# Cross attention with a sequential scan: the last block's queries transposed like the others', other due dates, and a changed path for the last 256 rows

## The chip, the cores and the metric

The kernel runs on one core of one Trainium2 chip, in a single launch. The metric is the device time of one execution in microseconds (us), as a median over runs. A profiled execution is a further run, with a time of its own. The core's engines are TensorE (PE in the profile; PEld are its weight loads), VectorE (DVE), ScalarE (ACT), GpSimd (POOL) and SyncE (SP), whose queue issues nearly all DMA transfers.

## The reference

`x` has 4096 rows and `ctx` 3202 rows of 512 float32 values; there are 8 heads of 64 and a state of 64. Cut to what matters:

```python
x1 = x + mha(LN1(x), LN1(ctx))             # 8 heads, softmax(q k / 8) v, then W_o and b_o
U  = (LN2(x1) @ W_in.T + b_in) @ Bmat      # 4096 x 64
s  = 0
for t in range(4096):
    s = silu(s @ A.T) + U[t]
    states[t] = s
out = x1 + states @ Cmat + (mean(ctxb) @ W_prog.T + b_prog)
```

## The kernel before

**Preparation.** The context is normalised in chunks, multiplied with the weights of keys and values, and the results are put into DRAM (`kd`, `vd`, lines 577 to 678), from where each unit of attention loads what it needs.

**Units of attention.** The 4096 queries form 8 blocks `Q` of 512. A unit is a block, a pair of heads `hp` and a `half` of 256 queries: 64 units, numbered 0 to 63. In the first seven blocks the two halves of a pair follow each other; in the last block all four pairs of one half come before those of the other, and keys and values are loaded again for each unit. A unit runs over 13 blocks of 256 keys. For each of these TensorE makes scores (16 small matmuls, L706), ScalarE takes the exponential of them with a shift (L783), VectorE adds the result into a running sum (L791) and TensorE multiplies it with the values (16 matmuls, L840). The scores go through a ring of two PSUM tiles, the exponentials through a ring of 18 SBUF tiles, the products into a single PSUM tile. So the work on TensorE is a row of half-steps, scores and products in turn. A unit ends with a copy of the products (L885, ScalarE), a join with what came before (L889, VectorE), a folding of the sums (L798, L810, L815), the sums over keys (L868, TensorE), their copy (L907), the reciprocal (L912) and the scaling (L923), and with the row operations L777 and L915 that belong to the choice of the shift.

**Queries.** `queries()` (L993) loads a block's rows, normalises them (factors on GpSimd, scaling on ScalarE, L981) and transposes them in one of two ways. For blocks 1 to 6 (`mixes(Q)`, L1074) VectorE transposes 32 x 32 squares (the flip, L1057) and four moves per half, each of four DMAs on SP's queue (L1069, 32 KB each), bring the squares to their places. For block 0 and block 7 TensorE transposes (the turn, L296, 8 matmuls for each half), and ScalarE copies the result from PSUM (L319). Either way the products with the query weights follow (heads, L325).

**Rows.** `project()` (L1094) works on a finished block by halves: load x, add a row of biases on GpSimd (row, L1110), product with W_o (outs, L1116), residual (L1129), statistics and scaling, flip, move, the product that gives U (inputs, L1172) and its copy (L1181). The inputs of a half need the moved block, so TensorE waits there for a DMA. A further GpSimd operation adds the constant row of `mod` (L1133).

**Tail.** The scan runs in chunks, in two sweeps. The second, `b`, has 16 steps of a product (z, L1281, TensorE), a tanh (L1309, ScalarE) and a sum (h, L1316, VectorE), which makes the states (L1348) and their products with Cmat (L1355), copied, added and stored (L1369 to L1380). The last 256 rows are finished only here. `last_rows()` (L1441) has their own chain: residual (L1457), statistics (L259, L261), factors (three GpSimd operations, L268 to L272), scaling (L280, ScalarE), turn (L296, L1472), copy (L1477), inputs (L1482), 20 serial steps of z, tanh and h (L1281, L1518, L1521), states (L1530), products with Cmat (L1565) and output (L1568). Beside it run checks: `differ()` (L1394 to L1407) compares two sweeps' states, `risen` looks at the shifts, `counted` and `number` (L1741) make of them a number that decides whether a general path is run afterwards; for these inputs it isn't.

**What sets the order.** The order of instructions on each engine is made when the program is built, by the class `Plan` (L69): every piece is added with an engine, an estimated cost, the pieces after which it may stand, a due date and the buffers that it takes and gives. A list scheduler puts them into one order by these. `SHIFT` (L82) moves the due dates of some kinds of pieces by so many times `STEP`, about one pair of half-steps. `from_(d)` (L957) names the piece of scores that is due at `d`; a piece that stands "after" it is only ordered behind it. On the chip an instruction waits for the data and buffers that it uses, and for what stands ahead of it on its engine.

```python
def mixes(Q):
    return 0 < Q < NQB - 1
```

Of the kernel before, what the change touches and what calls it, by code (L numbers as in the profile page):

```python
# [33 lines left out]
FIRST = 3  # L34
EPS = 1e-5
# [33 lines left out]
class Plan:  # L69
# [114 lines left out]
def xattn_ssm_kernel(  # L184
# [772 lines left out]
    def from_(d):  # L957

        return ("scores", *divmod(min(int(d / STEP), len(steps) - 1), NDC))
# [33 lines left out]
    def queries(plan, Q, d):  # L993

        copied, w = [], {}
        of_xn = ("query", Q, 0, "move0") if mixes(Q) else ("queries", Q, 0, "turn")
        for half in range(2):
            ks = [("query", Q, half * 2 + t) for t in range(2)]
            at = [Q * QB + half * QU + t * P for t in range(2)]
            k2, v = ("queries", Q, half), {}  # L1000
# [6 lines left out]
            for t in range(2):  # L1007
# [5 lines left out]
                             [] if mixes(Q) else [free] * 2, [from_(d + 8 * STEP)])  # L1013
# [10 lines left out]
            def turn(half=half, nv=nv, at=at, v=v, open_=open_):  # L1024
                open_()
                xn = w["xn"][:, :, half * QU : (half + 1) * QU]
                v["turns"] = [turned(xn, nv[t]["xh"], t, f"x{at[t]}") for t in range(2)]
                for one in v["turns"]:
                    next(one)

            after = [of_xn] if half else []
            takes = [] if half else ["xn"]
            if mixes(Q):
                for t in range(2):
                    plan.add((*ks[t], "flip"), "DVE", 720,
                             lambda t=t, v=v, nv=nv: flip(v["x"], nv[t]["xh"], t),
                             [(*k, "scaled") for k in ks], d + 4 * STEP + t, [], [("xh", (*ks[0], "scaled"))])
                for a in range(P // TB):
                    plan.add((*ks[0], f"move{a}"), "SP", 2600, partial(move_, a),
                             [(*k, "flip") for k in ks] + ([(*ks[0], "move0")] if a else after),  # L1040
                             d + (5 + 4 * a) * STEP, [] if a else takes, [free])
                    copied.append((*ks[0], f"move{a}"))
            else:
                plan.add((*k2, "turn"), "PE", 1050, turn, [(*k, "scaled") for k in ks] + after, d + 4 * STEP,
                         ["m", "m"] + takes, [("xh", (*ks[0], "scaled"))])
                for t in range(2):
                    plan.add((*ks[t], "copy"), "ACT", 560, lambda t=t, v=v: next(v["turns"][t], None),
                             [(*k2, "turn")], d + 5 * STEP + t, [], [("m", (*k2, "turn"))])
                    copied.append((*ks[t], "copy"))
# [24 lines left out]
    def mixes(Q):  # L1074
        return 0 < Q < NQB - 1
# [18 lines left out]
    def project(plan, Q, halves, d, index):  # L1094

        for half in halves:
# [157 lines left out]
    def open_scan():  # L1254
# [13 lines left out]
        for name, n in (  # L1268
            ("end0", NCK + 1), ("end1", NCK + 1), ("ul", PRE + 1 + P), ("hw", P), ("hl", P),
            ("sl", P + 1), ("df", NCK), ("thl", P // LT), ("st", P // LT),  # L1270
            ("top", 1), ("low", 1), ("bad", 1), ("badl", 1), ("badr", 1),
        ):
            sv[name] = two[:, at_ : at_ + n]
            at_ += n
# [116 lines left out]
    def largest(new):  # L1391

        top, low = sv["top"], sv["low"]
        nc.vector.tensor_reduce(top, new, AX.X, ALU.max, apply_absolute_value=True)  # L1394
        nc.vector.tensor_scalar(low, top, -TOL, None, ALU.mult)
        nc.vector.tensor_scalar(top, top, TOL, None, ALU.mult)

    def differ(new, old, n, bad):

        top, low, df, ok = sv["top"], sv["low"], sv["df"][:, :n], sv["ok"][:, :n]  # L1400
        nc.vector.tensor_tensor(df, new, old, ALU.subtract)
        nc.vector.tensor_scalar(ok, df, top, None, ALU.is_le)
        yield
        nc.vector.scalar_tensor_tensor(ok, df, low, ok, ALU.is_ge, ALU.mult)
# [36 lines left out]
    def last_rows(plan, d):  # L1441

        n = len(units) - 1
        v = dict(x1={}, xh={}, tp={}, pu={}, fs={})
# [87 lines left out]
        for g in range(2):  # L1532
# [4 lines left out]
            plan.add(("l.stats", g), "DVE", 870, partial(stats_, g), [("l.x1", g)], d + g)  # L1537
            plan.add(("l.factors", g), "POOL", 1100, partial(factors_, g), [("l.stats", g)], d + g)
            plan.add(("l.scaled", g), "ACT", 800, partial(scaled_, g), [("l.factors", g)], d + g)
# [11 lines left out]
        for t in range(PRE + LT):  # L1551
# [3 lines left out]
            plan.add(("l.h", t), "DVE", 180, partial(h_, t), [("l.tanh", t)], d)  # L1555
        plan.add("l.from", "DVE", 180, from_, [("l.h", PRE)], d + 7 * STEP)
# [17 lines left out]
    def neighbours():  # L1574

        sl = sv["sl"]
        nc.vector.tensor_copy(sl[:NS, 0:1], sv["end0"][NS:, END : END + 1])
        nc.vector.tensor_copy(sl[NS:, 0:1], sl[:NS, P:])
# [64 lines left out]
    def drain(plan):  # L1643
# [18 lines left out]
        plan.add("start", "SP", 0, ready_scan, ["fetch", ("sums", n)], d - 2 * STEP, ["s"])  # L1662
        plan.add("yb", "SP", 0, ready_rows, [("den", n - 1, 1)], a0, ["m", "m"])
        plan.add("py1", "SP", 0, ready_py, ["start", ("rise", n)], d, ["s"])
# [21 lines left out]
        plan.add("close", "SP", 0, close, [("l.x1", g) for g in range(2)] + ["py1", ("join", n)] + ended, d - 16 * STEP)  # L1686
# [21 lines left out]
        for name, new, old, count, bad, of in (  # L1708
            ("b", lambda: sv["end0"][:, 1:], lambda: sv["end1"][:, 1:], NCK, "bad", [("b", "end")]),
            ("l", lambda: sv["sl"][:, : P : LT], lambda: sv["st"], P // LT, "badl",  # L1710
             ["l.near", "l.from", ("differ", "b", 2)]),
# [9 lines left out]
            costs = (1250, 500, 440) if count == NCK else (900, 300, 350)  # L1721
            for i in range(3):
                plan.add(("differ", name, i), "DVE", costs[i],
# [3 lines left out]
        def risen():  # L1727
            bad = sv["badr"]
            nc.vector.tensor_scalar(rises, rises, RISE, None, ALU.is_le)
            nc.vector.tensor_reduce(bad, rises, AX.X, ALU.add, negate=True)  # L1730
            nc.vector.tensor_scalar(bad, bad, 3.0 * len(units), None, ALU.add)
# [7 lines left out]
        def number():  # L1739
            sv["nbad"] = small.tile([1, 1], I32, tag="nbad", name="nbad")  # L1740
            nc.vector.tensor_copy(sv["nbad"], sv["py"][1][0][0:1, 0:1])  # L1741
# [4 lines left out]
        plan.add("l.near", "DVE", 320, neighbours, ["l.states", ("b", "end")], d)  # L1746
# [247 lines left out]
```

## Time and profile before

| | us |
|---|---|
| median of three runs | 1957.63 |
| lowest and highest run | 1956.58, 1958.08 |
| profiled execution, its time | 1960.71 |
| profiled execution, its span | 1958.9 |

The mean granted clock of TensorE in the profiled execution was 0.996. The span is what the profiler's records cover. In a row of a timeline stand the start in us from the span's start, the length, the engine, the line, the operation, output and inputs with their sizes, and the number of instructions drawn together; at its end, in brackets, the idle time ahead of it and what ended that. Matmuls overlap, so starts tell more than lengths. In a row of a group the figures after the bar are the busy time in us, the mean length of one in ns, then the idle time ahead and its releasers.

### The profile page before, as it was taken

To read this page: it belongs to the slowest core of one execution; us is meant where nothing else is said; L and a number is where in the kernel's file an instruction comes from. 1 tells how busy PE (TensorE), PEld (TensorE's weight loads), DVE (VectorE), ACT (ScalarE), POOL (GpSimd) and SP (SyncE) were. 2 spreads that over 40 slices of the span, in tenths; PEclk is the share of its full clock that TensorE was granted. 3 is DMA by queue.
4 is the path that set the end of the run, shared out by engine and by line. 5 is a ranking of instruction groups with operands and counts; after the bars stand their busy time and mean duration, and the time that the engine had idled before them with its cause. 6 is when DMAs were issued, how large, how long until landed. Compare 5 with 4: busy or idle time off the path is not lost. (4 is left out here: it accounts for less than half of the span.)

```text
span 1958.9 us, 66935 instructions
## 1 busy us (share of the span) xinstructions
PE 1928.9 (98%) x29092; PEld 1259.3 (64%) x29092; DVE 1459.3 (74%) x1983; ACT 1171.3 (60%) x1632; POOL 225.5 (12%) x374
## 2 busy tenths in 40 slices
PE   9999999999999999999999999999999999999996
PEld 5444577666667666666667666666666666766674
DVE  4321489688878887888868886888778886877876
ACT  2233477566666666666657665666666675665653
POOL 2111000001200120011100120012001100011105
PEclk9999999999999999999999999999999999999998
DMA  6533234123422243223312342224322331544476
GB/s 195 172 102 108 64 85 115 48 86 88 129 79 80 86 114 84 74 83 109 104 47 86 92 121 77 81 87 122 87 82 75 95 96 43 156 134 141 143 207 199
DMA packets 246935, 204.28 MB, mean 104 GB/s; under 512 B 80809, under 2 KB 220073, under 8 KB 246637
## 3 DMA queue, kind: packets, MB, share of 16 engines
q1 hardware_dynamic: 242616, 193.32, 34.1%
q10 hardware_dynamic: 4020, 6.62, 1.1%
q8 instruction: 231, 3.78, 0.8%
q14 instruction: 68, 0.55, 0.1%
HBM read 156.32 MB, written 29.88 MB: 95 GB/s over the span
## 5 line engine op out<-in xcount | busy, mean ns | idle before, releaser
L783 ACT ACTIVATE p<-s,shifts 128x1024 f32<-128x1024 f32 (+1 forms) x832 | 890.1, 1081 | 482.9 <-PE s L706 474.3
L791 DVE TENSOR_TENSOR acc<-p,acc 128x1024 f32<-128x1024 f32 (+1 forms) x704 | 830.5, 1180 | 203.6 <-ACT p L783 169.8
L840 PE MATMUL po<-p,v 64*64 64x256 f32 x12800 | 834.1, 377 | 2.7 <-DVE o L889 2.5
L706 PE MATMUL s<-q,k 64*64 64x256 f32 x12800 | 834.9, 377 | 1.8 <-ACT p L783 1.8
L706 PEld LDWEIGHTS s<-q,k 64*64 64x64 f32 x12800 | 490.4, 133 | 214.2 <-issue 13.3
L840 PEld LDWEIGHTS po<-p,v 64*64 64x64 f32 x12800 | 485.0, 133 | 192.6 <-issue 12.0
L1110 POOL TENSOR_TENSOR xr<-xr,rowb 128x512 f32<-128x512 f32 x30 | 42.7, 1436 | 984.9 <-DMA xr<-in_x_dram 984.9
L912 DVE RECIPROCAL rd<-rd 128x256 f32<-128x256 f32 (+1 forms) x64 | 110.2, 1722 | 13.0 <-ACT rd L907 12.7
L325 PE MATMUL pq<-xn,wq 128*128 128x512 f32 x248 | 110.7, 598 | 0.0
L1116 PE MATMUL pa<-wo,o 128*128 128x512 f32 x240 | 107.0, 599 | 0.0
L623 PE MATMUL pv<-wv,ct 128*128 128x512 f32 (+1 forms) x208 | 92.6, 595 | 0.9 <-DVE wv L406 0.9
L656 PE MATMUL pk<-ct,wk 128*128 128x512 f32 (+1 forms) x224 | 88.9, 550 | 0.0
L575 DVE COPY ct<-tp_c 128x512 f32<-128x512 f32 (+1 forms) x13 | 8.4, 649 | 105.7 <-PE tp_c L296 105.7
L791 DVE TENSOR_TENSOR acc<-p,p 128x1024 f32<-128x1024 f32 x64 | 78.1, 1221 | 10.6 <-ACT p L783 10.6
L325 PEld LDWEIGHTS pq<-xn,wq 128*128 128x128 f32 x248 | 45.7, 190 | 55.5 <-issue 54.3
L1116 PEld LDWEIGHTS pa<-wo,o 128*128 128x128 f32 x240 | 44.4, 190 | 56.0 <-issue 55.5
L815 DVE TENSOR_TENSOR acc<-swap,acc 64x256 f32<-64x256 f32 x126 | 60.5, 480 | 11.1 <-ACT swap L810 9.4
L656 PEld LDWEIGHTS pk<-ct,wk 128*128 128x128 f32 x224 | 39.2, 190 | 42.6 <-issue 42.6
L623 PEld LDWEIGHTS pv<-wv,ct 128*128 128x128 f32 (+1 forms) x208 | 36.8, 186 | 43.4 <-issue 41.1
L664 ACT ACTIVATE ks<-pk,bias 128x512 f32<-128x512 f32 (+1 forms) x28 | 18.0, 642 | 74.7 <-PE pk L656 67.6
L810 ACT COPY swap<-acc 64x256 f32<-64x256 f32 x126 | 50.9, 404 | 16.9 <-DVE acc L798 14.4
L334 ACT ACTIVATE q<-pq,bias 128x512 f32<-128x512 f32 x31 | 21.3, 688 | 62.5 <-PE pq L325 62.5
(222 smaller groups left out, 1217.9 us busy)
## 6 DMA issues: line engine op xcount, KB each, us to landing
k<-kd SPq DMA_DIRECT2D x432, 128.0 KB, 2.3
v<-vd SPq DMA_DIRECT2D x432, 128.0 KB, 2.1
xn<-x SPq DMA_DIRECT2D x416, 32.0 KB, 1.9
xr<-in_x_dram SPq DMA_DIRECT2D x30, 256.0 KB, 3.5
x1d<-xr SPq DMA_DIRECT2D x30, 256.0 KB, 2.2
x<-in_x_dram SPq DMA_DIRECT2D x28, 256.0 KB, 3.2
cx<-in_ctx_dram SPq DMA_DIRECT2D x25, 256.0 KB, 3.3
vd<-vs SPq DMA_DIRECT2D x25, 256.0 KB, 2.4
```

The costliest lines, as they stand in the source:

```text
L325: nc.tensor.matmul(pq, wq[:, i, hp * P : (hp + 1) * P], xn[:, i, :], start=(i == 0), stop=(i == NC - 1),)
L623: nc.tensor.matmul(pv[h * HD : h * HD + n, :H], ct[:, k, o : o + n], wv[:, k, :], start=(i == 0), stop=(i == NC // parts - 1), skip_group_ ...
L656: nc.tensor.matmul(pk[:, :n_g], wk[:, i, hp * P : (hp + 1) * P], ct[:, i, :n_g], start=(i == 0), stop=(i == NC - 1),)
L706: nc.tensor.matmul(s[k0 : k0 + HD, a, b, :], kts[(*w["at"][:2], c)][r, b * CK + k0 : b * CK + k0 + HD], q[r], start=True, stop=True, skip_ ...
L783: nc.scalar.activation(t[:, :, :nb, :], w["ps"][c][:, :, :nb, :], AF.Exp, bias=w["shift"])
L791: nc.vector.tensor_tensor(w["acc"][:, :, :nb, :], t[:, :, :nb, :], before[:, :, :nb, :], ALU.add)
L810: nc.scalar.copy(w["swap"][r], of[(1 - k) * HD : (2 - k) * HD])
L815: nc.vector.tensor_tensor(of[r], w["swap"][r], of[r], ALU.add)
L840: nc.tensor.matmul(w["po"][a * HD : (a + 1) * HD, k, :QU], vts[Q, hp, c][r, b, a * HD : (a + 1) * HD], t[r, a, b, :], start=(c == 0 and b ...
L912: nc.vector.reciprocal(w["rd"][:, part], (w["pd"] if last else w["rd"])[:, part])
L1110: nc.gpsimd.tensor_tensor(v["x"], v["x"], rowb, ALU.add)
L1116: nc.tensor.matmul(v["pa"], o_t[Q, c, half][:, t * P : (t + 1) * P], wo[:, c, :], start=(c == 0), stop=(c == NC - 1),)
```

## The change

1. `queries()`: the last block's queries take the way of blocks 1 to 6, a flip on VectorE and moves by DMA. Its turn on TensorE and its copies on ScalarE are gone. The last unit's sums (L868) and the last block's other operations on queries read the mixed order accordingly.
2. `project()`: the row addition on GpSimd may stand no earlier than two steps ahead of its old due date, except for the last rows.
3. `last_rows()`: the statistics add EPS on VectorE, the factors are a single power on GpSimd, and VectorE does the scaling with mean and factor as its two scalars, where ScalarE had done it.
4. `last_rows()`: after each of the last three of the 20 serial steps' products (17, 18, 19) TensorE makes two products of 128 x 128 that nobody reads (`l.idle`).
5. The checks: `differ()` takes the absolute value on ScalarE instead of a comparison from both sides; `neighbours` becomes two copies on ScalarE; `risen` and `number` lose an operation each. Pieces that only allocate buffers (`start`, `yb`, `py1`, `close`) are put with VectorE in the plan.
6. `SHIFT` has other values and more kinds. Kinds that belong to a unit get a name ending in `.l` for the last two units (62 and 63), so that those can be dated by themselves.

```diff
+WARM = 17
+    UNIT = ("add", "inverse", "scale", "fall", "join", "output", "sums", "den", "swap", "gather", "fold", "rest")
+    ENDS = 2 * NC * NQB - 2
     SHIFT = {
-        "row.store": 16.5, "fold": 6.75, "rows.outs": 1, "heads": -12.25, "sample": -3, "spread": 5.75,
-        "query.flip": 10.25, "states": -11.5, "inverse": 7.5, "extra": 4, "scale": -13.25, "rest": 3.25,
-        "row.mod": -1.5, "joined0": -6,
+        "row.store": 11.5, "fold": 2, "rows.outs": 0.75, "heads": -12, "sample": -3, "spread": 4.75,
+        "query.flip": -11, "states": -5.5, "inverse": 4.75, "extra": 10, "scale": -57.75, "rest": -1,
+        "row.mod": -17, "joined0": -14.25, "b": -15, "add.l": -23, "l.stats": -34.75, "last": -4.5,
+        "base": -34.75, "inverse.l": -27, "rows.inputs": 3.5, "maximum": -13.5, "fall": -19, "query.stats": -8,
+        "den": 4.5, "row.scaled": 12, "l.h": -7, "row.stats": -9.25,
     }
...
+        elif sort in self.UNIT and name[1] >= self.ENDS:
+            sort += ".l"
...
-                        w["acc"][:, a, b, :],
+                        rows_of(w, w["acc"][:, a, b, :], True),
...
-            else:
-                plan.add((*k2, "turn"), "PE", 1050, turn, [(*k, "scaled") for k in ks] + after, d + 4 * STEP,
-                         ["m", "m"] + takes, [("xh", (*ks[0], "scaled"))])
-                for t in range(2):
-                    plan.add((*ks[t], "copy"), "ACT", 560, lambda t=t, v=v: next(v["turns"][t], None),
-                             [(*k2, "turn")], d + 5 * STEP + t, [], [("m", (*k2, "turn"))])
+            for t in range(2):
+                plan.add((*ks[t], "flip"), "DVE", 720,
+                         lambda t=t, v=v, nv=nv: flip(v["x"], nv[t]["xh"], t),
+                         [(*k, "scaled") for k in ks], d + 4 * STEP + t, [], [("xh", (*ks[0], "scaled"))])
+            for a in range(P // TB):
+                plan.add((*ks[0], f"move{a}"), "SP", 2600, partial(move_, a),
+                         [(*k, "flip") for k in ks] + ([(*ks[0], "move0")] if a else after),
+                         d + (5 + 4 * a) * STEP, [] if a else takes, [free])
...
     def mixes(Q):
-        return 0 < Q < NQB - 1
+        return Q > 0
...
-                plan.add((*ks[t], "row"), "POOL", 1270, partial(row, vs[t]), [(*ks[t], "load")], d - STEP)
+                plan.add((*ks[t], "row"), "POOL", 1270, partial(row, vs[t]),
+                         [(*ks[t], "load")] + ([] if last else [from_(d - 2 * STEP)]), d - STEP)
...
     def differ(new, old, n, bad):
         nc.vector.tensor_tensor(df, new, old, ALU.subtract)
+        yield
+        nc.scalar.activation(df, df, AF.Abs)
+        yield
         nc.vector.tensor_scalar(ok, df, top, None, ALU.is_le)
-        yield
-        nc.vector.scalar_tensor_tensor(ok, df, low, ok, ALU.is_ge, ALU.mult)
-        yield
-        nc.vector.tensor_reduce(bad, ok, AX.X, ALU.add, negate=True)
-        nc.vector.tensor_scalar(bad, bad, float(n), None, ALU.add)
+        nc.vector.tensor_reduce(bad, ok, AX.X, ALU.add)
...
         def stats_(g):
-            v["fs"][g] = stats(v["x1"][g], P, f"yl{g}")
+            mv = v["mv"][g] = stats(v["x1"][g], P, f"yl{g}")
+            rstd = v["fs"][g] = ln.tile([P, 1], F32, tag="rstd", name=f"rstd_yl{g}")
+            nc.vector.tensor_scalar(rstd, mv[:, 1:2], EPS, None, ALU.add)
         def factors_(g):
-            v["fs"][g] = factors(v["fs"][g], P, f"yl{g}")
+            nc.gpsimd.tensor_tensor(v["fs"][g], v["fs"][g], neg_half, ALU.pow)
         def scaled_(g):
-            v["xh"][g] = scaled(v["x1"][g], v["fs"][g], P, f"yl{g}")
+            xh = v["xh"][g] = ln.tile([P, H], F32, tag="xh", name=f"xh_yl{g}")
+            nc.vector.tensor_scalar(xh, v["x1"][g], v["mv"][g][:, 0:1], v["fs"][g], ALU.subtract, ALU.mult)
...
+        def idle_():
+            for k in range(2):
+                nc.tensor.matmul(sv["z"][1][:, k, :], a_t, a_t, start=True, stop=True)
+        for t in range(WARM, PRE + LT):
+            plan.add(("l.idle", t), "PE", 430, idle_, [("l.z", t), ("b", "h", L - 1)], d)
...
-    def neighbours():
-        nc.vector.tensor_copy(sl[:NS, 0:1], sv["end0"][NS:, END : END + 1])
-        nc.vector.tensor_copy(sl[NS:, 0:1], sl[:NS, P:])
+    def neighbour(g):
+        to, of = sv["sl"][g * NS : (g + 1) * NS, 0:1], (sv["end0"][NS:, END : END + 1], sv["sl"][:NS, P:])
+        nc.scalar.copy(to, of[g])
```

More of the change, by code (lines that the diff above doesn't have):

```diff
@@ L995, in queries @@
         copied, w = [], {}
-        of_xn = ("query", Q, 0, "move0") if mixes(Q) else ("queries", Q, 0, "turn")
+        of_xn = ("query", Q, 0, "move0")
         for half in range(2):
@@ L999, in queries @@
             at = [Q * QB + half * QU + t * P for t in range(2)]
-            k2, v = ("queries", Q, half), {}
+            v = {}
             def load(t, v=v, at=at):
@@ L1022, in move_ @@
                 move(w["xn"][:, :, half * QU : (half + 1) * QU], v["x"], a)
[L1024 to L1029, printed above, removed]
             after = [of_xn] if half else []
             takes = [] if half else ["xn"]
-            if mixes(Q):
-                for t in range(2):
[L1035 to L1042, printed above, removed]
-            else:
-                plan.add((*k2, "turn"), "PE", 1050, turn, [(*k, "scaled") for k in ks] + after, d + 4 * STEP,
-                         ["m", "m"] + takes, [("xh", (*ks[0], "scaled"))])
-                for t in range(2):
-                    plan.add((*ks[t], "copy"), "ACT", 560, lambda t=t, v=v: next(v["turns"][t], None),
-                             [(*k2, "turn")], d + 5 * STEP + t, [], [("m", (*k2, "turn"))])
-                    copied.append((*ks[t], "copy"))
+            for t in range(2):
[6 more added lines that the diff above has]
+                         d + (5 + 4 * a) * STEP, [] if a else takes, [free])
+                copied.append((*ks[0], f"move{a}"))
             d += 2 * QSTEP
@@ L1685, in drain @@
         ended = [("row", Q, t, "kept") for Q, n_ in ((NQB - 2, NT), (NQB - 1, NT // 2)) for t in range(n_)]
-        plan.add("close", "SP", 0, close, [("l.x1", g) for g in range(2)] + ["py1", ("join", n)] + ended, d - 16 * STEP)
+        plan.add("close", "DVE", 0, close, [("l.x1", g) for g in range(2)] + ["py1", ("join", n)] + ended, d - 16 * STEP)
         def products_(j, part):
@@ L1719, in first @@
                 next(v["d"])
[L1721 removed]
+            costs = (720, 280, 640) if count == NCK else (560, 200, 440)
             for i in range(3):
[L1723 removed]
+                plan.add(("differ", name, i), "ACT" if i == 1 else "DVE", costs[i],
                          partial(lambda v, *_: next(v["d"], None), v) if i else first,
@@ L1745, in drain @@
         plan.add("number", "DVE", 150, number, ["counted"], d)
-        plan.add("l.near", "DVE", 320, neighbours, ["l.states", ("b", "end")], d)
+        plan.add(("l.near", 0), "ACT", 190, partial(neighbour, 0), [("b", "end")], d)
+        plan.add(("l.near", 1), "ACT", 190, partial(neighbour, 1), ["l.states"], d)
         plan.add("l.ys", "PE", 1200, partial(last_ys, "a"), ["l.states"], d, ["mt"])
```

32 lines of the change are left out of this document (15 added, 17 removed).

## The prediction

> **What bounds the kernel now.** The list of busy times was read first, then TensorE's waits.
>
> ```profile
> PE 1928.9 (98%) x29092; PEld 1259.3 (64%) x29092; DVE 1459.3 (74%) x1983; ACT 1171.3 (60%) x1632; POOL 225.5 (12%) x374
> PE pu L1172 <- DMA xn<-x: 4.2, 2, 3.2
> PE py_o L1281 <- DVE scan L1521: 3.4, 3, 1.6
> PE po L840 <- DVE o L889: 2.5, 3, 1.2
> PE s L706 <- ACT p L783: 1.8, 7, 0.3
> ```
>
> TensorE works in 1928.9 of the span's 1958.9 us, so some 30 us of it are idle; time is won by taking work off TensorE or by closing one of its waits. The wait rows are line waited at, releaser, us in total, times, longest. The largest belongs to L1172, the rows' product that needs a transposed block brought by DMA. Where in the span the idle time lies is shown by the windows (length, busy us of PE, its weight loads, DVE, ACT and POOL with counts, granted clock, DMA share, GB/s):
>
> ```profile
> 1323.00:1372.00 49.00, 48.74 (x800) 32.13 (x796) 42.22 (x57) 32.91 (x48) 11.31 (x16) 1.00 0.44 123
> 1372.00:1421.00 49.00, 49.00 (x756) 31.84 (x752) 37.09 (x47) 29.95 (x43) 0.00 (x0) 1.00 0.33 87
> 1908.70:1920.00 11.30, 8.77 (x89) 5.47 (x92) 5.43 (x17) 4.25 (x10) 5.38 (x10) 1.00 0.47 138
> 1920.00:1938.40 18.40, 17.10 (x300) 12.91 (x298) 13.67 (x38) 9.50 (x31) 14.90 (x20) 1.00 0.76 251
> 1938.40:1949.00 10.60, 4.93 (x80) 3.26 (x75) 9.45 (x28) 2.92 (x10) 5.07 (x6) 0.89 0.80 268
> 1949.00:1959.00 10.00, 2.30 (x10) 0.71 (x10) 3.01 (x13) 0.00 (x0) 0.00 (x0) 0.50 0.31 107
> ```
>
> In mid-kernel TensorE is full (48.74 and 49.00 of 49.00). From 1908.7 to 1949.0 it idles 2.5 + 1.3 + 5.7 = 9.5 us: there the serial chain of the last 256 rows sets the pace, and after it 10 us of output follow.
>
> **1. The last block's queries go another way: -2.7 us.** Removed are two TensorE pieces of 8 transposes each and four ScalarE copies; added are four VectorE flips and eight moves, that is 32 issues on SP.
>
> ```profile
> 1554.47 1.24 PE L840 MATMUL po<-p,v 64*64 64x256 f32 x16
> 1555.63 1.09 PE L296 MATMUL tp_x<-ident,xh_x 128*128 128x128 f32 x8
> 1557.57 1.04 PE L840 MATMUL po<-p,v 64*64 64x256 f32 x16
> 1609.77 1.04 PE L706 MATMUL s<-q,k 64*64 64x256 f32 x16
> 1610.63 1.04 PE L840 MATMUL po<-p,v 64*64 64x256 f32 x16
> 1611.61 1.09 PE L296 MATMUL tp_x<-ident,xh_x 128*128 128x128 f32 x8
> 1613.55 1.04 PE L840 MATMUL po<-p,v 64*64 64x256 f32 x16
> L1057 DVE STREAM_TRANSPOSE x<-xh_x 128x512 f32<-128x512 f32 x24 | 15.8, 691 | 0.1
> xn<-x SPq DMA_DIRECT2D x416, 32.0 KB, 1.9
> ```
>
> A half-step (16 matmuls of scores or of products) takes 1610.63 - 1609.77 = 0.86 us from start to start. Product to product with a turn between takes 1557.57 - 1554.47 = 3.10 and 1613.55 - 1610.63 = 2.92, without it 1.72: 1.38 + 1.20 = 2.6 us, and with one change of array mode fewer 2.7 (2.2 to 2.9, from 2 x 1.09 up). It goes in whole from TensorE's path. The flips cost 4 x 0.69 = 2.8 us of VectorE, the moves run on SP and the DMA engines. Both are covered by TensorE's own work: both full windows hold such flips and moves for earlier blocks (the row with 16 GpSimd instructions the rows' work too), and TensorE lost 0.26 us in the two. Without that cover a flip would hold an addition up by 0.69 us, 2.8 us in all: the part would be worth nothing.
>
> **2. The wait at L1172: -4.9 us.**
>
> ```profile
> 1802.03 2.52 SPq L1069 DMA_DIRECT2D xn<-x  x4
> 1802.14 1.04 PE L840 MATMUL po<-p,v 64*64 64x256 f32 x16
> 1806.39 1.78 PE L1172 MATMUL pu<-xn,wc 128*64 128x128 f32 x16 [3.21 <-DMA xn<-x]
> 1808.10 1.99 PE L706 MATMUL s<-q,k 64*64 64x256 f32 x16
> 1809.86 1.14 PE L840 MATMUL po<-p,v 64*64 64x256 f32 x16
> ```
>
> SP issues the block's last move by 1802.03 + 2.52 = 1804.55; 1.9 us of landing later is 1806.4, when L1172 starts. The product stood too early by 3.21 us. What the wait cost is more: from 1802.14 to 1809.86 are 7.72 us, for 0.86 of products, 1.0 of L1172 and 0.86 of scores; beside those 2.7 us 5.0 are lost, 3.2 of them idle and 1.8 because the next groups ran long (1.78 and 1.99 instead of 1.04). In the changed order this L1172 stands six and a half half-steps later, 6.5 x 0.86 = 5.6 us, while its moves keep their place in SP's queue. So it comes 2.4 us after its data: I take 4.9 off (0 if SP is late by more than that). The same wait of the block before, 4.2 - 3.2 = 1.0 us, keeps its order and stays. What is late next is nothing on TensorE: the result only feeds the scan in the tail, a hundred us on.
>
> **3. The other dates: -0.8 us.**
>
> ```profile
> 419.55 0.41 DVE L889 TENSOR_TENSOR o<-po,o 128x256 f32<-128x256 f32 x1
> 420.01 1.09 PE L840 MATMUL po<-p,v 64*64 64x256 f32 x16 [1.17 <-DVE o L889]
> L791 DVE TENSOR_TENSOR acc<-p,acc 128x1024 f32<-128x1024 f32 x640 | 786.5, 1229 | 199.6 <-ACT p L783 169.0 <-DVE acc L791 0.9
> L783 ACT ACTIVATE p<-s,shifts 128x1024 f32<-128x1024 f32 (+1 forms) x832 | 890.1, 1081 | 482.9 <-PE s L706 474.3
> ```
>
> The joins (L889) free the single product tile; three times a product waits for them, 2.5 us. At every eighth unit the join now stands behind one more addition (1.23 us) and two short row operations (together about 2.0 us), and the product that needs it comes two half-steps and a short group (about 1.9 us) later: 0.1 at each of seven places, +0.6. The seven waits of scores for the exponential (1.8 us) sat mostly where two scores stood one half-step apart; these places are gone (-1.6), and similar spacings come at other places, where the like cost nothing before (+0.2). Sum -0.8. The low end is all the waits of L840 and L706 gone, -4.3; the high end +4, the joins' 1.23 us uncovered at three or four of the seven places.
>
> **4. The tail: -2.8 us.**
>
> ```profile
> 1909.87 0.22 POOL L268 TENSOR_SCALAR ve_yl<-mv_yl 128x1 f32<-128x1 f32 x1 [21.73 <-DVE mv_yl L261]
> 1910.84 0.26 POOL L272 TENSOR_SCALAR nmr_yl<-mv_yl,rstd_yl 128x1 f32<-128x1 f32 x1
> 1912.66 0.81 ACT L280 ACTIVATE xh_yl<-x_l,nmr_yl,rstd_yl 128x512 f32<-128x512 f32 x1 [0.37 <-POOL nmr_yl L272]
> 1914.01 0.44 PE L1281 MATMUL z<-scan,a_t 64*64 64x128 f32 x4 [0.91 <-DVE scan L1316]
> 1914.38 0.66 PE L296 MATMUL tp_yl<-ident,xh_yl 128*128 128x128 f32 x4
> L406 DVE TENSOR_SCALAR wq<-raw_q,g1s 128x512 f32<-128x512 f32 x4 | 1.7, 481 | 1.5 <-DMA raw_q<-in_L_xattn_W_qkv_dram 1.5
> 1941.88 0.36 DVE L1402 TENSOR_SCALAR scan<-scan 128x128 f32<-128x128 f32 x1
> 1942.22 1.26 POOL L1372 TENSOR_TENSOR row<-y_l,row 112x512 f32<-112x512 f32 x1
> 1942.27 1.35 DVE L1404 SCALAR_TENSOR_TENSOR scan<-scan 128x128 f32<-128x128 f32 x1
> 1949.02 1.19 PE L1565 MATMUL py_a<-c,scan 64*128 64x512 f32 x1 [1.40 <-DVE scan L1530]
> 1951.11 0.69 DVE L1568 SCALAR_TENSOR_TENSOR xr_l<-py_a,xr_l 128x512 f32<-128x512 f32 x1 [0.16 <-PE py_o L1565]
> ```
>
> The last rows' statistics pass three GpSimd operations (1909.87 to 1911.10), then ScalarE; the second half is scaled at 1912.66 + 0.81 = 1913.47, and the turn follows at 1914.38, behind the sweep's step at 1914.01. Without two of the GpSimd operations (0.22 and 0.26 with their gaps, 0.7) and with VectorE's 0.48 (L406's shape) for 0.81, less 0.2 for the added EPS, the scaling ends some 0.8 us earlier, and the turn now stands two steps of the sweep ahead (1.1 to 1.3 us each): about 2 us earlier. I pass 2.0 on to the end, since the chain has waits all the way (the sum of idle above); 0 is the other end, because TensorE is 93% busy from 1920 to 1938.4.
> The check whose 1.35-us operation holds a step's L1521 up (the wait row with 3.4 us, longest 1.6) is shorter and two steps later, but its Abs now stands ahead of a step's tanh on ScalarE: -0.4 (0.7 to 0).
> The dummy products: the four last products run from 1949.02 to 1951.1, 2.1 us, at a granted clock of 0.50 in that window. At full clock they would take half, -1.0; the window before them stood at 0.89 and its dummies are six only, so I take -0.4 (0 to -1.0).
> VectorE's scaling of the second half may run beside GpSimd's 512-wide operation on the last rows. The row at 1942.27 shows such a pair: 1.35 us, where a single-input operation of that size took 0.36: up to +1.0, which I leave in the bounds. [...]
> [...]
> Tail: -2.0 - 0.4 - 0.4 = -2.8 (-4.5 to +1). The row adds' gate is a rule for the order alone and leaves GpSimd's order nearly as it was: 0; they are hidden by TensorE's work, GpSimd being busy 12%.
>
> **The sum:** -2.7 - 4.9 - 0.8 - 2.8 = -11.2. The profiled execution took 1960.71 us around its span of 1958.9, 3.1 above the median of the runs, 1957.63; it would become 1949.5, its span 1947.7. On the median: 1946.4.
>
> **Rivals.** *A, the stall stays:* SP's 32 new issues at 0.63 us (2.52 for 4) delay the moves in front of L1172 by over 2.4 us, the wait moves along. For: SP's transfers are what ended the wait. Against: their order is the same. 1946.4 + 4.9 = 1951.3.
> *B, the tail gives nothing:* the earlier chain meets the full stretch from 1920 to 1938.4, or VectorE's scaling collides. For: 93% there. Against: 5.7 idle us behind it. 1949.2. *A and B:* 1954.1.
> *C, slower: ScalarE takes over.* The new dates put more than 1.3 us of other work between two exponentials at 48 places, 33 before. An exponential takes 1.08 us and TensorE gives it 1.72; without slack such a place costs 1.3 + 1.08 - 1.72 = 0.66 us, 48 x 0.66 = 32, less the 1.8 there already: 1977. It is slower than before from (11.2 + 3.9) / 48 = 0.31 us a place. For: only two score tiles lie between the engines. Against: at 33 such places there were seven waits, 1.8 us, 0.05 a place, and ScalarE idles 482.9 / 832 = 0.58 us before each exponential.
> *D, more comes off:* the joins' and scores' waits go whole and the tail gives 4.5: about 1942.
>
> **How the numbers follow.** Forecast 0.45; A 0.15; B 0.14; both 0.08; C 0.10; D 0.08. The range reaches from D's end, 1941, over A and B to 1955; outside are C and the worst of both. A measurement of this kernel tells some 0.2% (3.9 us) from no change: faster means below 1953.7. Faster 0.45 + 0.15 + 0.14 + 0.08 = 0.82, same 0.08 (A and B), slower 0.10.
>
> **What would show it.** Right: no L296 among the last block's queries; no wait at L1172 over 1.0 us; the waits of L706 for L783 under 2 us; the last rows' turn about 2 us nearer to the end of their statistics; idle time of TensorE from 30 to some 24 us, its busy time down by 5. Wrong: an L1172 that still waits 3 us; a hundred short waits at L706; a last-rows scaling over 1 us; a clock still at 0.50 in the last four products.

## The result, and the profile after

| us | before | after |
|---|---|---|
| median of six runs each | 1959.12 | 1947.70 |
| lowest to highest | 1956.58 to 1964.93 | 1946.32 to 1949.57 |
| profiled execution, span | 1958.9 | 1947.8 |

The ratio is 0.9936, 95% interval 0.9924 to 0.9947: 12.5 us less of 1959, where 11.2 were forecast (1946.4 against 1947.7). The sum was right; two of its four terms were not. The page's first row and TensorE's waits of the changed kernel follow. Line numbers differ from kernel to kernel: in the changed one L713 is the L706 of before (scores), L790 is L783 (exponential), L835 is L828 (the products of the last two keys), L847 is L840 (products), L896 is L889 (join), L1165 is L1172 (the rows' inputs), L1274 is L1281 (the sweep's steps).

```profile
PE 1927.4 (99%) x29088; PEld 1259.5 (65%) x29088; DVE 1465.8 (75%) x1982; ACT 1169.8 (60%) x1630; POOL 216.5 (11%) x370
PE po L835 <- issue: 1.7, 1, 1.7
PE z L1274 <- DVE scan L1309: 1.6, 3, 1.2
PE pu L1165 <- DMA k<-kd: 1.4, 1, 1.4
PE py_a L1566 <- DVE scan L1524: 1.2, 1, 1.2
PE py_o L1466 <- DVE xh_yl L1460: 0.9, 1, 0.9
PE py_o L1274 <- DVE scan L1515: 0.5, 2, 0.4
PE s L713 <- ACT p L790: 0.2, 1, 0.2
```

The wait of 3.2 us for moved rows is gone, the other one stayed (1.4 us, over the 1.0 that the prediction allowed; it names a load of keys as the last to come, but the group reads moved rows alone); the joins' waits are gone altogether, the exponentials' nearly. New are a wait of 1.7 us at L835 that names no releaser, and 0.9 us for the last rows' scaling. The idle time fell from 30.0 to 20.4 us, the busy time by 1.5 only. Where the span's 11.1 us went is read from places that both traces have, the start of a unit's first scores (after minus before, in us):

| unit 0 | unit 50 | unit 57 | unit 60 | unit 62 | unit 63 | last VectorE operation |
|---|---|---|---|---|---|---|
| +0.75 | -4.54 | -8.27 | -8.23 | -13.18 | -13.13 | -10.86 |

So units 0 to 49 gave 5.3 (the dates), 50 to 56 3.7 (the turns, and a date), 60 and 61 4.95 (the wait), and from unit 63 on 2.3 were lost. The preparation ahead of unit 0 took 0.75 more in this execution. The tail, in windows of the changed kernel with the columns of before:

```profile
1897.00:1908.60 11.60, 9.44 (x58) 5.45 (x62) 7.61 (x21) 2.24 (x6) 4.57 (x6) 0.85 0.69 178
1908.60:1927.00 18.40, 17.02 (x288) 12.70 (x290) 12.43 (x37) 8.62 (x30) 11.95 (x17) 1.00 0.59 192
1927.00:1937.60 10.60, 9.26 (x139) 6.79 (x130) 9.15 (x27) 4.72 (x17) 6.92 (x9) 1.00 0.96 325
1937.60:1948.00 10.40, 1.62 (x12) 0.55 (x10) 3.33 (x11) 0.42 (x2) 1.06 (x1) 0.68 0.45 148
```

The granted clock is up longer at the end (0.68 in the last window, for 0.50), but down at the tail's start (0.85), where it had been 1.00.

### The profile page after: what moved, and what is told of

It reads as the page before. It is cut to its first block, busy times and chain, and to the rows that moved or that the text cites. A ratio compares the mean times of both kernels' runs of the same rounds, so it can differ in the third digit from the quotient of the medians.

```text
span 1947.8 us, 66909 instructions
## 1 busy us (share of the span) xinstructions
PE 1927.4 (99%) x29088; PEld 1259.5 (65%) x29088; DVE 1465.8 (75%) x1982; ACT 1169.8 (60%) x1630; POOL 216.5 (11%) x370
## 4 chain that ended last, share of the span: by engine, by line
## 5 line engine op out<-in xcount | busy, mean ns | idle before, releaser
L790 ACT ACTIVATE p<-s,shifts 128x1024 f32<-128x1024 f32 (+1 forms) x832 | 891.8, 1081 | 479.7 <-PE s L713 465.1
L713 PE MATMUL s<-q,k 64*64 64x256 f32 x12800 | 833.6, 377 | 0.2 <-ACT p L790 0.2
L847 PE MATMUL po<-p,v 64*64 64x256 f32 x12800 | 832.6, 377 | 0.0
L713 PEld LDWEIGHTS s<-q,k 64*64 64x64 f32 x12800 | 488.6, 133 | 208.1 <-ACT p L790 15.0
L847 PEld LDWEIGHTS po<-p,v 64*64 64x64 f32 x12800 | 485.0, 133 | 193.4 <-issue 16.9
L822 DVE TENSOR_TENSOR acc<-swap,acc 64x256 f32<-64x256 f32 x126 | 55.3, 439 | 8.9 <-ACT swap L817 7.2
L784 DVE TENSOR_TENSOR acc<-x,acc 2x256 f32<-2x256 f32 x128 | 53.0, 414 | 2.6
```

The lines of the kernel that those rows point to most:

```text
L713: nc.tensor.matmul(s[k0 : k0 + HD, a, b, :], kts[(*w["at"][:2], c)][r, b * CK + k0 : b * CK + k0 + HD], q[r], start=True, stop=True, skip_ ...
L784: nc.vector.tensor_tensor(to[r], t[r], to[r], ALU.add)
L790: nc.scalar.activation(t[:, :, :nb, :], w["ps"][c][:, :, :nb, :], AF.Exp, bias=w["shift"])
L822: nc.vector.tensor_tensor(of[r], w["swap"][r], of[r], ALU.add)
L847: nc.tensor.matmul(w["po"][a * HD : (a + 1) * HD, k, :QU], vts[Q, hp, c][r, b, a * HD : (a + 1) * HD], t[r, a, b, :], start=(c == 0 and b ...
```

## The experiments

In runs 1, 4, 6, 7 and 9 to 11 the finished order was edited: `put(pieces, behind)` takes pieces out of the planned list and puts them behind another one.

**1. The kernel before, one product later.**

```diff
+        put([("rows", 6, 1, "inputs"), ("row", 6, 2, "kept"), ("row", 6, 3, "kept")], ("scores", 61, 0))
```

> The kernel before with one piece put elsewhere in the order: the last L1172 group (with the copies of its result) stands behind the first scores of unit 61 instead of ahead of scores 10 of unit 60. Theory: the wait of 3.21 us goes and the half-clocked groups behind it with it, -4.9 us by the start of unit 62, nothing before unit 60 changes; span 1954.0. Rival A of the prediction: the moves arrive later still or the stall goes elsewhere, then -0 to -2. A rival for the size: only the idle 3.21 goes and the long groups behind it (1.7) stay, -3.2.

The waits:

```profile
PE pu L1179 <- DMA xn<-x: 1.7, 1, 1.7
```

and the timeline of TensorE:

```profile
1809.87 1.04 PE L713 MATMUL s<-q,k 64*64 64x256 f32 x16
1810.84 1.09 PE L1179 MATMUL pu<-xn,wc 128*64 128x128 f32 x16
```

One wait is left, of the first half of the block, and the moved group starts with none. Against the kernel before, unit 60 starts 1.89 us later (waits ahead of it that the edit doesn't touch), unit 62 3.01 earlier: -4.90. The long groups behind the wait went with it. The span is 1956.4, above the 1954.0 expected, since unit 60 came late; by the medians the kernel is 3.0 us faster (1958.04 for 1961.03), ratio to before 0.9981 (0.9967 to 0.9996).

**2. The kernel before, queries of the last block flipped** (`queries()`, `mixes()` and L868 as in the diff).

> The kernel before with the last block's queries on the way of the others (flips and moves), all dates as before. Theory: -2.6 us between the starts of units 50 and 57 (two turns of about 1.1 us with a change of array mode on each side), and no change before unit 49; with the old dates the flips and moves fall later than in the changed kernel, and the last L1172 still waits about 3 us. Rival: the eight moves collide with other work of SP and the query products wait for them, so that less than 1.5 us comes off or time is lost.

Unit 50 starts 0.66 us earlier than before, unit 57 3.28: -2.62. The last L1172 still waits, as expected, for 2.5 us; not expected was a second wait, like the changed kernel's:

```profile
PE pu L1157 <- DMA xn<-x: 3.6, 2, 2.5
PE po L828 <- issue: 2.0, 1, 2.0
```

This wait of 2.5 us cost little more than its idle time, for the groups behind it are not long:

```profile
1802.37 1.09 PE L1157 MATMUL pu<-xn,wc 128*64 128x128 f32 x16 [2.51 <-DMA xn<-x]
1803.40 1.09 PE L706 MATMUL s<-q,k 64*64 64x256 f32 x16
```

The granted clock stayed at 1.00 here. In the kernel before, where these two groups took 1.78 and 1.99 us, it fell just behind the wait of 3.2 us (windows with the columns of the prediction):

```profile
1803.22:1806.63 3.41, 0.24 (x4) 0.27 (x6) 2.27 (x4) 0.62 (x1) 0.00 (x0) 1.00 0.41 92
1806.64:1810.05 3.41, 3.41 (x36) 2.36 (x36) 0.00 (x0) 0.95 (x2) 0.00 (x0) 0.50 0.74 237
```

So the long groups are the clock's, and not every long wait has them. From unit 63 to the last operation 3.6 us are given back (-5.64 to -2.00). Ratio 0.9984 (0.9972 to 0.9996).

**3. The changed kernel, fold at its old date.**

```diff
-        "row.store": 11.5, "fold": 2,
+        "row.store": 11.5, "fold": 6.75,
```

> The changed kernel with the old due date of one kind, the folding of the sums (6.75 instead of 2 steps later). Theory: the earlier folding let the reciprocal, the scaling and the row operation finish ahead of the join, so that the product tile came free in time; with the old date the join stands behind them again and TensorE waits for it at most of units 8, 16, 24, 32, 40, together 1.5 to 3 us, and the kernel is 2 to 4 us slower than the changed one. Rival: the waits went because the first product of units 8k stands two half-steps later; then the waits stay at zero here and the time stays within 1 us of the changed kernel's.

The first of its waits:

```profile
PE s L713 <- ACT p L790: 2.0, 8, 0.3
```

No wait at L847 for L896 is left in its waits. That doesn't settle the theory, for the old date doesn't put the reciprocal, the scaling and the row operation behind the join again. At the first of the places they are done by 416.5 as in the changed kernel, and the join follows:

```profile
416.11 0.41 DVE L922 TENSOR_REDUCE rises<-rd 128x1 f32<-128x256 f32 x1
420.43 0.42 DVE L896 TENSOR_TENSOR o<-po,o 128x256 f32<-128x256 f32 x1
```

So their early place doesn't come from the fold's date. The old date brings back the scores' waits instead, in place and size (0.3 us in one unit of each of seven blocks), and units 0 to 49 give 2.7 instead of 5.3. The median is 1949.42, the ratio to before 0.9946 (0.9928 to 0.9964): by the runs it isn't told apart from the changed kernel.

**4. The kernel before, first products of units 8, 16, ... 48 later.**

```diff
+        for u in range(8, 56, 8):
+            put([("product", u, 0), ("product", u, 1)], ("scores", u, 6))
```

> The kernel before with one thing moved: the first two groups of products of units 8, 16, 24, 32, 40 and 48 stand behind the scores of key block 6, where the changed kernel has them. Theory after the run with the old fold date: this place alone closes the join's waits; the waits of L840 for L889 go from 2.5 us to below 0.2, and the start of unit 49 comes 2 to 2.5 us earlier. Rival: the wait only moves to the scores or to the exponentials behind (a group of scores then stands right behind another), and less than 1 us is gained.

The waits, and the timeline of TensorE around unit 8's first products:

```profile
PE s L714 <- ACT p L791: 4.0, 13, 0.4
```

```profile
416.91 1.91 PE L714 MATMUL s<-q,k 64*64 64x256 f32 x32
419.19 2.10 PE L714 MATMUL s<-q,k 64*64 64x256 f32 x32 [0.37 <-ACT p L791]
421.11 2.12 PE L848 MATMUL po<-p,v 64*64 64x256 f32 x36
```

Half of each: the join's waits are gone, as the theory had it, and scores wait for exponentials in their place, 0.37 us at each of the places, as the rival had it; unit 49 gains nothing. In the changed kernel a group of products stands between the scores of blocks 3 and 4 and a short group (`sample`) between 5 and 6. The place of the products alone doesn't pay; that it pays together with this spacing of the scores is argued from the two orders, the spacing alone wasn't run.

**5. The changed kernel again, and a third time.** No edit.

> The changed kernel once more, for two things in its last unit. In its first profile TensorE stood idle for 1.69 us in the middle of a group of the extra products (L835) with no releaser named, and the granted clock fell to 0.50 for about 2.5 us behind the last rows' turn. If these belong to the order (theory: a wait for a buffer; two short waits of 2.1 us together let the clock fall), both come again within 0.3 us of the same place. If they belong to the one execution (rival: loading of instructions, the phase of the clock's control), one or both are gone and the span is 1.5 to 3 us shorter than 1947.8.

> The changed kernel on the same chip as the three that follow, to tell the execution's luck from the order. The wait at L835 has been 1.7, 1.2 and, in two kernels that differ from it only behind that place, 0.2 and 0.0 us; the clock fell behind the last rows' turn only where that wait was over 1 us. Theory: both vary with the chip and the execution: span 1943 to 1948, and where the wait at L835 is under 0.3 us, the mean granted clock is 0.999 and the span under 1944.5.

Spans 1948.7 in both, a little over the expected; median 1947.85 of the third's six runs. The wait at L835 was 1.15 and 1.01 us. The clock stood at 0.50 for 6.8 us behind the last rows' turn in both, where the first profile had 3.4. Both things came again at their places, in other sizes: the order has a part in them, and so has the execution.

**6. The tail's loads held back.**

```diff
+        def hold():
+            rows[4] = sp_.tile([P, 2, H], F32, tag="s", name="row_4")
+            nc.vector.memset(rows[4][:, :, 0:1], 0.0)
+        plan.add("hold", "DVE", 0, hold, [("product", n, 2)], d + 8 * STEP)
+        put(["hold"] + [("fetch", j) for j in range(4, 16)], ("fall", 61))
```

> The changed kernel, but the tail's loads of finished rows (32 issues of 224 and 256 KB) stop after the first eight until VectorE has done the row operation of unit 61, some 19 us later (one tiny memset of the next row tile makes that load wait). In the profiles so far the wait at L835 ends 1.4 to 1.6 us after a 16-KB packet of the queue that carries TensorE's instructions, and the DMA engines are over 100% busy with those rows from some 10 us into unit 63 on. Theory: TensorE runs out of instructions, because their packets queue behind the rows; with the loads held back the wait at L835 (1.2 to 1.7 us) is below 0.3 us and the first score of unit 63 to the last L835 takes 1.2 to 1.7 us less. Rival: the products wait for data or a buffer; then the wait stays. The rows may come too late for the joined outputs behind: up to +3 us at the end.

The DMA queues in some 8 us ahead of the wait in the changed kernel, and in the 14 us up to the same place here (packets, MB, share of 16 engines):

```profile
q1 hardware_dynamic: 1012, 1.83, 105.6%
```

```profile
q1 hardware_dynamic: 767, 1.37, 38.2%
q8 instruction: 2, 0.03, 1.1%
```

The first shows the rows' queue alone: no packet of the queue that the page calls instruction (q8) starts for 8 us while the rows fill the DMA engines (105.6%). Ahead of unit 63 these packets (16 KB) start 6.5 to 7.9 us apart. Counted from the start of unit 63, they start at 7.05, 19.83 and 28.14 us in the changed kernel, and at 7.63, 18.46, 22.36 and 27.96 here, where the wait is gone, as it is in the three kernels below that hold the loads back too. The granted clock stayed at 1.00 up to the last products (mean 0.999), and the span of this one execution is 1941.1.

**7. The last rows' `mod` behind the first two states.**

```diff
+        put([("l.mod", 0), ("l.store", 0), ("l.mod", 1), ("l.store", 1)], ("states", 1))
```

> The changed kernel with GpSimd's addition of the constant row to the last rows (two of 1.27 us) moved behind the first two states, so that it doesn't run beside VectorE's scaling. In the changed kernel the two scalings take 2.04 us together and the second turn waits 0.93 us for them. [...] Rival: a scaling takes 1.0 us by itself; nothing changes there. At the end of the kernel 0 to -0.9, since the middle of the tail is full.

Timelines of the changed kernel, then of this one:

```profile
1901.79 2.04 DVE L1460 TENSOR_SCALAR xh_yl<-x_l,mv_yl,rstd_yl 128x512 f32<-128x512 f32 x2
1902.27 2.68 POOL L1490 TENSOR_TENSOR xr_l<-x_l,modb 128x512 f32<-128x512 f32 x2
```

```profile
1901.14 1.22 DVE L1467 TENSOR_SCALAR xh_yl<-x_l,mv_yl,rstd_yl 128x512 f32<-128x512 f32 x2
1903.05 2.50 POOL L1497 TENSOR_TENSOR xr_l<-x_l,modb 128x512 f32<-128x512 f32 x2
```

Beside GpSimd the two scalings took 0.82 us more (the second alone 1.43 for 0.60), and the second turn came that much later. What the neighbour costs shows only in such a pair: the same instruction, with and without it.

**8. The old normalisation in the changed order** (bodies of `stats_`, `factors_`, `scaled_` as before).

> The changed kernel with the last rows' old normalisation (three GpSimd operations, ScalarE's scaling), the order otherwise as in the changed kernel: the new scaling's worth alone. Theory of the prediction: the second scaling ends 0.8 us later without it. What the profile of the changed kernel suggests: GpSimd's addition slowed the new scaling, so that only 0.2 to 0.5 us lie between the two at the second turn, and nothing at the last step of the serial chain. Rival: it is worth 0.8 us or more at the second turn and at the end of the chain.

From the first residual (L1448) to the second turn: 6.72 us before, 5.87 changed, 5.39 here, 5.05 in run 7. So the changed scaling brought the second turn 0.48 us later than the old one would have in this order: the order won 1.33 us there, the scaling gave 0.48 of them back, and 0.85 were left. To the first of the 20 serial steps' sums: 12.4, 12.2, 10.25, 10.4.

**9. The three together,** with L1165 of unit 59 four half-steps later.

```diff
+        put([("rows", 6, 0, "inputs"), ("row", 6, 0, "kept"), ("row", 6, 1, "kept")], ("product", 58, 11))
```

> The changed kernel with three pieces put elsewhere: the tail's row loads held back after eight issues until unit 61's row operation, GpSimd's additions for the last rows behind the first two states, and the L1165 group that waits 1.4 us for moved rows (unit 59) four half-steps later. Theory: no wait at L1165 over 0.3 us (-1.4 to -1.8), no wait at L835 (-0 to -1.7, as the other executions had it), second turn 0.8 us earlier than with the loads held back alone, which the middle of the tail passes on by 0.3: span 1938.5 to 1940, faster than the changed kernel by 3 to 7 us. Rival: the full tail gives the parts back, and the span is above 1941.

Median 1943.97 on the chip of the third run of the changed kernel (1947.85); ratios to before 0.9918 (0.9905 to 0.9931) and 0.9939 (0.9926 to 0.9952): faster than before, and by the medians 3.9 us faster than the changed kernel, though the intervals overlap. No wait at L1165 or L835; 0.5 us went to the scores behind L1165's new place, and the clock fell again behind the last rows' turn, to 0.50 for 3.4 us. The spans are 1940.5 to 1944.8, mostly above 1941: the expected 1938.5 to 1940 was missed, and the rival was nearer.

**10. The same without the dummy products.**

> The combined kernel without the six dummy products; the order is otherwise the same. Theory: the granted clock is at 0.50 when the last four products (L1566) run, which then take 2.1 us from the first's start to the first output's instead of 1.3, as in the kernel before: 0.8 us slower than the combined kernel. Rival: the clock stays up without them, since no wait of TensorE is longer than 1.3 us there, and the time is the same within 0.2 us.

The timeline of the last products and the first output:

```profile
1933.63 1.19 PE L1574 MATMUL py_a<-c,scan 64*128 64x512 f32 x1 [1.31 <-DVE scan L1533]
1934.61 1.05 PE L1574 MATMUL py_a<-c,scan 64*128 64x512 f32 x1
1935.70 0.69 DVE L1577 SCALAR_TENSOR_TENSOR xr_l<-py_a,xr_l 128x512 f32<-128x512 f32 x1 [0.69 <-PE py_o L1574]
```

The last products take 2.08 us to the first output, as before; with the dummies 1.30 in the changed kernel. But the 20 serial steps take 27.21 us without and 27.66 with them: they win 0.78 and cost 0.45. In the profile of run 9 they won less than they cost: the last products took 1.78 us there. Median 1945.09, not told apart from run 9.

**11. The same with the old normalisation.**

> The combined kernel with the last rows' old normalisation (three GpSimd operations and ScalarE). Theory: from the start of the first residual of the last rows to the end of the second scaling 5.3 us, as in the kernel before, where VectorE's new scaling takes 4.9 without GpSimd beside it: 0.4 us slower than the combined kernel. Rival: the new scaling is worth nothing even so, 0.

Second turn at 5.40 against 5.05 us after the first residual, as expected; the time isn't told apart from run 9 (1942.95, with GpSimd's additions still behind the states), so nothing of it shows at the end.

## Why the prediction was right, and where not

**1, the turns (-2.7): right.** -2.62 alone (run 2), the 2.6 of the rows; the 0.1 that the sum added for a change of array mode is shown by no run. The flips and moves were covered. In the changed kernel units 50 to 56 give 3.7, with the fold at its old date 2.9 (run 3).

**2, the wait at L1172 (-4.9): right,** -4.90 alone (run 1) and -4.95 in the changed kernel, against this profile of the kernel before. Of the 5.0 us, 1.8 are the clock's fall to 0.50 behind the wait, and that part needn't come with every wait: behind the 2.5 us in run 2 the clock stayed at 1.00.

**3, the other dates (-0.8): the right sign, far too small.** The first 50 units gave 5.3, beyond the low end of 4.3. The step that failed: "At every eighth unit the join now stands behind one more addition (1.23 us) and two short row operations (together about 2.0 us), and the product that needs it comes two half-steps and a short group (about 1.9 us) later: 0.1 at each of seven places, +0.6". In the first of the places, timelines of the changed kernel:

```profile
416.18 0.41 DVE L922 TENSOR_REDUCE rises<-rd 128x1 f32<-128x256 f32 x1
...
418.16 1.23 DVE L798 TENSOR_TENSOR acc<-p,p 128x1024 f32<-128x1024 f32 x1
...
420.29 0.42 DVE L896 TENSOR_TENSOR o<-po,o 128x256 f32<-128x256 f32 x1
421.32 2.77 PE L847 MATMUL po<-p,v 64*64 64x256 f32 x48
```

and the kernel before:

```profile
419.22 0.41 DVE L915 TENSOR_REDUCE rises<-rd 128x1 f32<-128x256 f32 x1
```

This trace is 0.33 us later at that point. So the join came 0.4 us later than before (419.55), while the product's turn came 2.1 later (before it was wanted at 420.01 - 1.17 = 418.84). The reciprocal with its scaling and row operation, which had ended at 419.63 right ahead of the join, was done by 416.59: three operations had moved out of the join's way, and the sum had only counted those that moved into it. So the joins gave their 2.5 us instead of costing 0.6. Run 4 shows that the product's later place alone closes these waits; whether the operations had to move too isn't shown. The scores' waits went as forecast (-1.6; back in run 3), but they were worth more, from start to start: at a place with a wait of 0.26 us the unit became 0.48 shorter, about 2.9 in all.

**4, the tail (-2.8): wrong sign,** +2.3 from unit 63 on. The wait at L835 and the clock's fall turned it: in runs 6, 7 and 8, with the clock at 1.00 there and a wait of 0.2 us at most, the same stretch gained 1.7, 1.6 and 1.1. Each of its terms:
- *The chain 2.0 us earlier.* The first turn did come 2.0 earlier after the first residual (4.28 us for 6.23), the second only 0.85, since VectorE's scaling ran beside GpSimd: the +1.0 that the prediction left in the bounds. Runs 7 and 8 show it: 0.82. At the first serial sum little was left: 12.2 us after the residual, 12.4 before. With the clock at 1.00 it came at 10.7 (run 6), without GpSimd beside the scaling at 10.4 (run 7): the clock took 1.5, rival B's collision 0.35. In the two repeats, with the clock at 0.50 for 6.8 us instead of 3.4, the sum came at 13.3. B's other cause, the full stretch, took nothing: the steps behind take 27.66 us in every one of these kernels.
- *The check's -0.4.* The 20 steps take 27.66 us, 27.49 before, but 0.45 of that belong to the dummies: without them they take 27.21 (run 10), 0.28 less than before. Whether that is the check's isn't shown; no run changes it alone.
- *The dummies' -0.4.* -0.78 at the end and +0.45 in the steps (run 10): -0.33, with the clock at 1.00 through the last products, as in the changed kernel.
- *Not in the sum:* unit 63 lost 2.1 us around L835 in the profiled execution, and 0.9 between its sixth and its last scores.

Rivals A and C are out: no wait at L1165 of unit 61, and the exponentials' waits fell from 1.8 to 0.2 us although 48 stretches of other work over 1.3 us stand between exponentials, 33 before. D's first half (joins and scores go whole) came true, its second not. The total agrees by luck: terms 3 and 4 missed by about 4.5 and 5 in opposite directions. The signs tell it too: the busy time was to fall by 5 us and fell by 1.5, as units 50 to 56 and 60 to 61 took 3.2 and 1.7 off it and the tail, with its fall of the clock, put 3.8 on; and a last-rows scaling took 1.43 us, where over 1 was named as a sign of being wrong. The tail's low end of -4.5 is more than its own terms give (-2.0, -0.7 and -1.0 are -3.7).

## What to carry to other kernels

Price a wait from start to start, over the groups behind it too, and look whether the clock fell there: that part (1.8 of 5.0 us here) may be missing in another execution. When an order changes, place both sides of a wait again in time, the releaser and the one who waits: work that moves ahead of the releaser while its engine would have been idle cost nothing here (the three operations ahead of the joins, whose 2.5 us of waits went). And a list of small gains in a serial tail is worth what is left when the tail's own limits have taken theirs: here an engine busy for 93% of a stretch, the clock at 0.50, a scaling 0.82 us longer beside another engine's addition, DMA engines at 105%.

## What the runs showed of the hardware

**A wait without a releaser, and the packets of instructions.** The wait sits in the middle of a group whose data had long been there:

```profile
1887.14 0.38 PE L835 MATMUL po<-x,vx 64*64 64x128 f32 x2
1887.26 0.38 PE L847 MATMUL po<-p,v 64*64 64x256 f32 x2
1889.34 0.34 PE L835 MATMUL po<-x,vx 64*64 64x128 f32 x3 [1.69 <-issue]
```

In seven executions with flipped queries and the loads as they were it took 2.0, 1.7, 1.15, 1.0, 0.9, 0.2 and 0 us; with the loads held back 0 in four; with the old turns 0 in three. q8's packet tells them apart. Counted from the start of unit 63 it starts at 26.9 to 28.1 us in the five with a wait of 0.9 us and more, at 26.3 and 26.7 in the two with less, at 22.4 to 23.3 with the loads held back, and at 23.7 to 24.8 with the old turns, though rows fill the DMA engines there too (104.9% in the kernel before). These packets go with TensorE's instructions: the changed kernel has 231 of 16 KB for 29088 matmuls and as many weight loads, one for every 252, and in its stretches from 196 to 392 and from 392 to 588 us they are 24 and 25, one for every 257 and 259. That TensorE stood still for want of instructions is the author's inference, from the packet, which ends 1.4 to 1.6 us ahead of the restart in the five traces with the long wait, and from run 6, where it comes earlier and the wait is gone. Why it starts earlier in the kernels with turns stays open.

**The clock fell in one of two executions of the same order.** In the traces of the kernel before and of the changed one the record of the granted clock starts 4.41 and 6.01 us after the span's start, and each later change comes a whole multiple of 3.413 us behind that: the falls at 528 and 569 times of it (1806.65 and 1946.59 us) and at 556 and 567 times (1903.82 and 1941.37 us). The first fall of each lasted 3.41 us, the second to the end of the trace; in the repeats of run 5 the clock was at 0.50 for 6.8 us. The record starts at another time in each of the two, so these windows need not cut an order at the same places. Here is the window ahead of the fall in run 9 and the one behind it, then the same two in run 10, whose order is the same up to there:

```profile
1897.81:1901.21 3.40, 2.06 (x18) 1.23 (x16) 2.43 (x7) 1.35 (x4) 1.72 (x4) 1.00 1.04 243
1901.22:1904.62 3.40, 3.40 (x26) 3.04 (x25) 1.21 (x5) 0.54 (x2) 2.15 (x2) 0.50 1.06 248
```

```profile
1897.30:1900.71 3.41, 2.06 (x16) 1.07 (x14) 2.69 (x8) 1.14 (x3) 1.66 (x5) 1.00 1.06 248
1900.72:1904.12 3.40, 3.19 (x38) 2.32 (x39) 2.11 (x6) 1.04 (x3) 2.43 (x2) 1.00 1.05 241
```

TensorE was busy for 2.06 us of both windows; one is followed by a fall, the other isn't. The dummies come 25 us later and can't be the reason. In the traces of the two kernels the windows ahead of the four falls had TensorE busy for 0.07 and 0.45 (before), 0.41 and 0.44 (changed) of their time. No fall followed those of 0.55, 0.59 and 0.60 (before) and of 0.50 and 0.58 (changed), while 0.61 came before the fall in run 9: in that range the share didn't tell a fall from none. No single wait ahead of them was as long as such a window: TensorE's longest was 3.21 us before and 1.69 in the changed kernel. What the clock answers to wasn't tried.
